# The first products of two kernel generators: three pixel blocks in three column tiles of TensorE, one relu for each three

## Chip, core and metric

The kernel runs on one core of one Trainium2 chip. The metric is the device time of one execution in microseconds. Three runs of the kernel before gave a median of 3211.7 us (3210.56 to 3212.76).

## What is computed

The input `x` is 4 images of 256 channels by 64 x 64 pixels, all in float32. Four layers follow one another, each `x = x + layer(group_norm(x))`: a 3 x 3 convolution with attention over all pixels (layer 0), linear attention (layer 1), a convolution whose weights are generated from the image itself (layer 2), and a mixture of four expert matrices (layer 3). Only the generators of layer 2 are touched here:

```python
def _gen_kernel(x, W1, b1, W2, b2):
    h = relu(einsum('bchw,rc->brhw', x, W1) + b1)     # 8 hidden rows, all 4096 pixels
    pooled = h.mean(axis=(2, 3))
    return pooled @ W2.T + b2
dk = _gen_kernel(x, Wd1, bd1, Wd2, bd2)               # 3x3 weights, one set per channel
pk = _gen_kernel(x, Wp1, bp1, Wp2, bp2)               # 256 x 256 mixing weights
```

The two generators have 8 hidden rows each, so `W1` of both together is 16 rows over 256 channels.

## The kernel before

A channel lies on a partition. 256 channels are two halves `h` of 128 partitions (`NH = 2`), and a half image is 128 x 4096 numbers. An image is worked through in 8 blocks of 512 pixels, the width of one PSUM bank.

The order of the instructions is written out by hand. Layer 0's attention is a generator, `attend` (L610 to L673): each of its steps issues two products `pf` (L620), two exponentials `pr` on ScalarE (L621), two products `py` (L659) that read the exponentials of the step before, and one running sum `tot` on VectorE (L109). What is left of the image before (its layers 1 to 3) and the next image's convolution form a second generator, a `Chain` (L39). `run` (L1096) takes one step of the chain and then one step of the attention, so that both lie in one another's gaps on every engine. A chain's part ends a stretch with `yield n`: about n times a rate makes one step. The rate is 1.5 for the first image's attention, 0.86 for the next two and 1.24 for the last. Images 0, 1 and 2 have their layers 1 to 3 beside the attention of images 1, 2 and 3. Image 3 has no attention left to lie beside: its tail runs alone at the end, with products of image 2's mixing (`held`) put into gaps.

The function touched is `generated` (L855 to L1000), which is layer 2. It scales the 16 columns of `W1` by the group norm's factor (`w1n`, L862), and makes the bias of the hidden rows by four tiny products into `ps_b1` (L866; the profile writes `ps_b`) and a subtraction (`b1n`, L868). Then it goes over 8 blocks of pixels:

```python
for c in range(N // 512):
    ps = bank("ps_h")
    for h in range(NH):
        nc.tensor.matmul(ps[0:2 * R, :], w1n[:, h, :], big[:, h, bass.ts(c, 512)], ...)
    nc.scalar.activation(junk()[0:2 * R, :], ps[0:2 * R, :], AF.Relu, bias=b1n, accum_out=hs[:, c:c + 1])
```

The relu's `accum_out` sums the block's 512 pixels into one column of `hs`. In the same round of the loop one piece of the image is normalised into `xin` (L889 on ScalarE; in the last image every second one is on VectorE, L887), and the round ends with `yield 0.5`. After the loop `hs` is summed to `pooled` (L892), set on the diagonal of `pd` (L894), spread over all partitions by a product with ones (`ps_pool`, L897), and turned into the 3 x 3 weights `dk` by three VectorE operations. These weights start the convolution: ScalarE writes its centre tap (`centre`, L914), and in the last image nine diagonal matrices (L969) before it; VectorE adds the eight other taps (`dw`, L112), and products `ps_pw` (L922) mix the channels.

In front of all that, at the kernel's start, SyncE issues the loads of the weights one after the other (`resident`, L142), GpSimd fills constants, and VectorE makes two averaging matrices (`block_average`, L175) between the statistics of the first image.

Of the kernel before, what the change touches and what calls it, by code (L numbers as in the profile page):

```python
# [8 lines left out]
F32 = mybir.dt.float32  # L9
AF = mybir.ActivationFunctionType  # L10
ALU = mybir.AluOpType
AX = mybir.AxisListType

P = 128
NH = 2
HW = 64
N = HW * HW
# [4 lines left out]
R = 8  # L22
# [11 lines left out]

TY, MY, TX, MX = 6, 4, 4, 2
IY, IX = HW // MY, HW // MX


class Chain:  # L39
# [42 lines left out]
def conv_preact_fast(ctx: ExitStack, tc: tile.TileContext, guard, x, wc, wtpg, ww, wqkv, wout, w1cat, wd2,  # L82
# [3 lines left out]
    nc = tc.nc  # L86
    B = x.shape[0]

    cp = ctx.enter_context(tc.tile_pool(name="const", bufs=1))
    wk = ctx.enter_context(tc.tile_pool(name="work", bufs=1))  # L90
    sp = ctx.enter_context(tc.tile_pool(name="small", bufs=2))
# [7 lines left out]
    def k2(name):  # L99
        return wk.tile([P, 512], F32, tag="k2", name=name, bufs=6)  # L100

    def junk():
        return wk.tile([P, 512], F32, tag="junk", name="junk")

    def bank(name):
        return pp.tile([P, 512], F32, tag="bank", name=name, bufs=8)

    def tt(o, a, b, op):
        nc.vector.tensor_tensor(o, a, b, op)  # L109
# [9 lines left out]
    big = cp.tile([P, NH, N], F32, name="big")  # L119
# [3 lines left out]
    theta, phi, g = tpg[:, 0, :], tpg[:, 1, :], tpg[:, 2, :]  # L123
# [18 lines left out]
    def resident(name, src):  # L142
        t = cp.tile(list(src.shape), F32, name=name)
        nc.sync.dma_start(out=t, in_=src)
        return t
# [8 lines left out]
    ww_s = resident("ww_s", ww)  # L154
    wqkv_s = resident("wqkv_s", wqkv)
    wout_s = resident("wout_s", wout)
    w1_s = resident("w1_s", w1cat)
    b1_s = resident("b1_s", b1cat)
    wd2_s = resident("wd2_s", wd2)
    bd2_s = resident("bd2_s", bd2)  # L160
    rw1_s = resident("rw1_s", rw1)
# [6 lines left out]
    ident = cp.tile([P, P], F32, name="ident")  # L168
    make_identity(nc, ident)
    ones = cp.tile([P, P], F32, name="ones")  # L170
# [4 lines left out]
    def block_average(name, k):  # L175

        member = sp.tile([P, P // k], F32, name=name + "_m", bufs=1)
        nc.vector.tensor_reduce(member, ident.rearrange("p (g k) -> p g k", k=k), AX.X, ALU.add)
        t = cp.tile([P, P], F32, name=name)
        nc.vector.tensor_scalar(t.rearrange("p (g k) -> p g k", k=k),  # L180
                                member.unsqueeze(2).to_broadcast([P, P // k, k]), 1.0 / k, None, ALU.mult)
        return t

    avg32 = block_average("avg32", HD)
    avg8 = block_average("avg8", 8)

    def rsqrt(o, v):
# [85 lines left out]
    def group_finish(st, avg, eps, shift=None):  # L273


        mv = sp.tile([P, NH, 2], F32, name="mv")
        for h in range(NH):
            nc.vector.bn_aggr(mv[:, h, :], st[:, h, :, :].rearrange("p c s -> p (c s)"))
        if shift is not None:
            tt(mv[:, :, 0], mv[:, :, 0], shift, ALU.add)  # L280
        yield 1
        pm = bank("pm")
        nc.tensor.matmul(pm[:, 0:NH], avg, mv[:, :, 0], start=True, stop=True)
        gm = sp.tile([P, NH], F32, name="gm")
        nc.vector.tensor_copy(gm, pm[:, 0:NH])
        ev = sp.tile([P, NH], F32, name="ev")
        tt(ev, mv[:, :, 0], gm, ALU.subtract)
        tt(ev, ev, ev, ALU.mult)
        tt(ev, ev, mv[:, :, 1], ALU.add)
        yield 1  # L290
        pv = bank("pv")
        nc.tensor.matmul(pv[:, 0:NH], avg, ev, start=True, stop=True)
        rstd = sp.tile([P, NH], F32, name="rstd")
        nc.vector.tensor_scalar(rstd, pv[:, 0:NH], eps, None, ALU.add)  # L294
        rsqrt(rstd, rstd)
        return mv, gm, rstd
# [558 lines left out]
    def generated(w, b, big, k4, st, sh, diag):  # L855
        _, gm, rstd = yield from group_finish(st, avg8, 1e-5, sh)
        nb = norm_bias(gm, rstd, sh)
        off = sp.tile([P, NH], F32, name="off")
        tt(off, gm, sh, ALU.subtract)

        w1n = sp.tile([P, NH, 2 * R], F32, name="w1n")
        tt(w1n, w1_s, rstd.unsqueeze(2).to_broadcast([P, NH, 2 * R]), ALU.mult)  # L862
        yield 1
        pb1 = bank("ps_b1")
        for h in range(NH):
            nc.tensor.matmul(pb1[0:2 * R, 0:1], w1n[:, h, :], off[:, h:h + 1], start=(h == 0), stop=(h == NH - 1))  # L866
        b1n = sp.tile([2 * R, 1], F32, name="b1n")
        tt(b1n, b1_s, pb1[0:2 * R, 0:1], ALU.subtract)  # L868
        hs = sp.tile([2 * R, 8], F32, name="hs")
        pk = k2("pk")  # L870
        nc.sync.dma_start(out=pk, in_=bp2)

# [2 lines left out]
            nc.sync.dma_start(out=t, in_=wp2[:, bass.ts(j, 2), :])  # L875
            return t

        for c in range(N // 512):
            ps = bank("ps_h")
            for h in range(NH):  # L880
                nc.tensor.matmul(ps[0:2 * R, :], w1n[:, h, :], big[:, h, bass.ts(c, 512)],  # L881
                                 start=(h == 0), stop=(h == NH - 1))
            nc.scalar.activation(junk()[0:2 * R, :], ps[0:2 * R, :], AF.Relu, bias=b1n, accum_out=hs[:, c:c + 1])
            h, q = c % 2, c // 2
            normed = xin[:, h, bass.ts(q, CH // HW), :], big[:, h, bass.ts(q, CH)].rearrange("p (y x) -> p y x", x=HW)
            if diag is not None and h == 1:
                nc.vector.tensor_scalar(*normed, rstd[:, h:h + 1], nb[:, h:h + 1], ALU.mult, ALU.add)  # L887
            else:
                nc.scalar.activation(*normed, AF.Identity, bias=nb[:, h:h + 1], scale=rstd[:, h:h + 1])  # L889
            yield 0.5  # L890
        pooled = sp.tile([2 * R, 1], F32, name="pooled")
        nc.vector.tensor_reduce(pooled, hs, AX.X, ALU.add)  # L892
        pd = sp.tile([2 * R, 2 * R], F32, name="pd")
        nc.vector.tensor_scalar(pd, ident[0:2 * R, 0:2 * R], pooled, 1.0 / N, ALU.mult, ALU.mult)  # L894
        yield 1
        ppl = bank("ps_pool")
        nc.tensor.matmul(ppl[:, 0:2 * R], ones[0:2 * R, :], pd, start=True, stop=True)  # L897
        pb = sp.tile([P, 2 * R], F32, name="pb")
        nc.vector.tensor_copy(pb, ppl[:, 0:2 * R])
        dkp = k2("dkp")[:, 0:NH * 9 * R].rearrange("p (k r) -> p k r", r=R)  # L900
# [6 lines left out]
        rows = CH // HW  # L907
# [64 lines left out]
        for n, i in enumerate(mine):  # L972
# [15 lines left out]
            c, h = PARTS[i]  # L988
# [86 lines left out]
    def tail(b, big, qT, k4=k4, diag=None, xs_in=None, held=None):  # L1075

        def layers(w):
            st, sh = yield from nonlocal_out(w, b, big, k4, xs_in)
            st = yield from linear_attention(w, b, big, qT, k4, st, sh, diag is not None)
            st, sh = yield from generated(w, b, big, k4, st, sh, diag)  # L1080
            if b + 2 < B:
                load_x(b + 2)
            elif b + 2 == B:
                for h in range(NH):
                    for q in range(2):
                        half_image = bass.ts(q, N // 2)
                        nc.sync.dma_start(out=x_cols[:, h, half_image], in_=xs_d[b + 1, h, :, half_image])
            yield from mixed(w, b, big, k4, st, sh, held)
        return layers
# [557 lines left out]
@with_exitstack  # L1647
def conv_preact_kernel(ctx: ExitStack, tc: tile.TileContext, *args):
    nc = tc.nc
    B = args[0].shape[0]  # L1650
    gp = ctx.enter_context(tc.tile_pool(name="guard", bufs=1))
    guard = gp.tile([P, 2, B * NQ + 1], F32, name="guard")
    conv_preact_fast(tc, guard, *args)


    fit = gp.tile([P, 2, B * NQ + 1], F32, name="fit")
    for side in range(2):
        nc.vector.tensor_scalar(fit[:, side, :], guard[:, side, :], GUARD_MAX[side], None, ALU.is_le)
    low = gp.tile([P, 1], F32, name="low")
    nc.vector.tensor_reduce(low, fit.rearrange("p s k -> p (s k)"), AX.X, ALU.min)  # L1660
    every = gp.tile([P, P], F32, name="every")
    nc.gpsimd.memset(every, 1.0)
    good = gp.tile([P, 1], mybir.dt.int32, name="good")
    with tc.tile_pool(name="guard_ps", bufs=1, space=bass.MemoryType.PSUM) as gps:
        count = gps.tile([P, 1], F32, name="count")
        nc.tensor.matmul(count, every, low, start=True, stop=True)
        nc.vector.tensor_scalar(good, count, P - 0.5, None, ALU.is_ge)
    in_range = nc.values_load(good[0:1, 0:1], min_val=0, max_val=1)
    with tc.If(in_range < 1):
        conv_preact_general(tc, *args)  # L1670
# [58 lines left out]
```

## Time and profile before

| | |
|---|---|
| median of three runs | 3211.7 us |
| the profiled execution | 3210.14 us, of which its span is 3208.4 us |
| TensorE (PE) busy | 3071.0 us, 96% of the span |
| VectorE (DVE) busy | 2075.8 us, 65% |
| ScalarE (ACT) busy | 1146.0 us, 36% |
| GpSimd (POOL) busy | 129.4 us, 4% |
| mean granted TensorE clock | 0.986 of full |

A line of a group or of the timeline names the source line, the engine, the operation, what it writes and reads, and how many instructions were merged. A float32 product leaves two weight loads (PEld) and two matmul records (PE), one for each of two passes: the 64 products of `ps_h` show as 128 records. In a dense row the records of matmuls overlap (those of `ps_h` last 592 ns each and start 0.43 us apart), so what a pass occupies is read from the distance between starts. In the timeline, `[1.30 <-PE ps_h L881]` says that the engine had been idle for 1.30 us before the line, and what ended it. L109 and L112 are the helpers `tt` and `stt`, so that VectorE's work is told apart by the tile's name.

### The profile page before, as it was taken

The numbers are of one execution on the slowest core, as the hardware profiler recorded it, in microseconds if no ns is written. First come the engines' busy times: TensorE is split into PE (matmuls) and PEld (weight loads), VectorE is DVE, ScalarE is ACT, GpSimd is POOL, SyncE is SP. The second block draws the span as 40 slices with busy tenths as digits, with TensorE's granted clock in tenths as the row PEclk, the third lists the DMA queues.
The fourth block names the chain that finished last, engine by engine and source line by source line (L and its number), as shares of the span: only waits on it lengthen the run. The fifth ranks groups of instructions, "written<-read, shape, count | busy, mean of one in ns | idle before, by whom it ended". The sixth has DMA issues, their size and how long they took to land.

```text
span 3208.4 us, 24196 instructions
## 1 busy us (share of the span) xinstructions
PE 3071.0 (96%) x8494; PEld 1476.7 (46%) x8494; DVE 2075.8 (65%) x2603; ACT 1146.0 (36%) x2139; POOL 129.4 (4%) x169
## 2 busy tenths in 40 slices
PE   6899999999999999999999999999999999996797
PEld 3354444445564444444565444444555534443533
DVE  8636776443556986876537796878353768855575
ACT  2133224333555332223364432312355443333520
POOL 0000000000010000000011000000000100000100
PEclk9999999999999999999999999999999999998998
DMA  5510113001100023113200102210510010121101
GB/s 180 173 39 27 33 34 62 7 13 63 49 10 27 13 72 118 40 33 76 101 11 6 35 20 90 101 38 27 129 42 1 10 40 7 49 70 46 50 0 73
DMA packets 73792, 161.66 MB, mean 50 GB/s; under 512 B 7744, under 2 KB 39232, under 8 KB 70720
## 3 DMA queue, kind: packets, MB, share of 16 engines
q1 hardware_dynamic: 69056, 143.27, 13.1%
q0 software_dynamic: 4608, 16.78, 2.9%
q8 instruction: 69, 1.13, 0.2%
q14 instruction: 59, 0.48, 0.0%
HBM read 103.40 MB, written 73.40 MB: 55 GB/s over the span
## 4 chain that ended last, share of the span: by engine, by line
PE 79%; DVE 12%; issue 5%; ACT 2%; DMA 0%; POOL 0%; SPq 0%; POOLq 0%; ACTq 0%
PE pf L620 23%; PE py L659 23%; PE ps_conv L382 8%; PE ps_qkv L748 5%; DVE dw L112 4%; PE ps_tp L596 3%; PE ps_ex L1059 3%; PE ps_pw L922 2%; DVE tot L109 2%; PE ps_g L601 2%; PE ps_h L881 2%; PE ps_wy L643 2%; PE ps_o L813 1%; PE ps_ctx L768 1%; PE ps_ss L735 1%
## 5 line engine op out<-in xcount | busy, mean ns | idle before, releaser
L621 ACT ACTIVATE pr<-pf 128x512 f32<-128x512 f32 x1024 | 604.1, 596 | 1227.7 <-PE pf L620 1203.7
L620 PE MATMUL pf<-tpg 128*128 128x512 f32 x2048 | 968.7, 595 | 1.4 <-ACT pr L621 1.4
L659 PE MATMUL py<-pr,tpg 128*128 128x512 f32 x2048 | 962.1, 592 | 3.0 <-ACT pr L621 2.9
L109 DVE TENSOR_TENSOR tot<-tot,pr 128x1024 f32<-128x1024 f32 x448 | 546.5, 1220 | 263.3 <-ACT pr L621 261.7
L659 PEld LDWEIGHTS py<-pr,tpg 128*128 128x128 f32 x2048 | 388.8, 190 | 494.2 <-issue 478.3
L620 PEld LDWEIGHTS pf<-tpg 128*128 128x128 f32 x2048 | 381.6, 190 | 447.3 <-issue 419.2
L112 DVE SCALAR_TENSOR_TENSOR dw<-xp,dk,dw 128x1008 f32<-128x1008 f32 x224 | 283.1, 1268 | 7.0 <-ACT dw L914 3.7
L382 PE MATMUL ps_conv<-v,u 128*128 128x512 f32 x576 | 260.7, 599 | 12.7 <-issue 9.0
L382 PEld LDWEIGHTS ps_conv<-v,u 128*128 128x128 f32 x576 | 110.3, 192 | 154.0 <-issue 147.0
L748 PE MATMUL ps_qkv<-wqkv_s,xg 128*128 128x384 f32 x384 | 130.7, 490 | 0.0
L596 PE MATMUL ps_tp<-big,wtpg_s 128*128 128x512 f32 x256 | 116.8, 599 | 3.0 <-ACT big L471 3.0
L189 POOL TENSOR_TENSOR rstd<-rstd,half 128x2 f32<-128x2 f32 x24 | 16.8, 701 | 2478.8 <-DVE rstd L294 2285.2
L109 DVE TENSOR_TENSOR tpg<-ps_g,bg_s 128x512 f32<-128x512 f32 x32 | 22.1, 692 | 144.3 <-PE ps_g L601 144.3
L922 PE MATMUL ps_pw<-dw,pk 128*128 128x512 f32 x224 | 103.8, 597 | 10.9 <-DVE dw L112 10.9
L634 DVE RECIPROCAL inv<-pss 128x512 f32<-128x512 f32 x32 | 107.2, 3351 | 7.3 <-PE pss L632 7.3
L748 PEld LDWEIGHTS ps_qkv<-wqkv_s,xg 128*128 128x128 f32 x384 | 72.2, 190 | 52.5 <-issue 8.9
L756 DVE TENSOR_REDUCE qs<-qk 128x16 f32<-128x512 f32 x24 | 16.5, 686 | 123.4 <-ACT qk L750 123.4
L109 DVE TENSOR_TENSOR v<-ra 128x1024 f32<-128x1024 f32 x72 | 86.7, 1220 | 0.4
L597 ACT ACTIVATE tpg<-ps_tp,btp_s 128x512 f32<-128x512 f32 x64 | 43.7, 686 | 118.4 <-PE ps_tp L596 118.4
L922 PEld LDWEIGHTS ps_pw<-dw,pk 128*128 128x128 f32 x224 | 42.7, 191 | 65.4 <-issue 50.9
L596 PEld LDWEIGHTS ps_tp<-big,wtpg_s 128*128 128x128 f32 x256 | 47.5, 193 | 54.3 <-issue 49.8
L750 ACT ACTIVATE qk<-ps_qkv,rinv 128x256 f32<-128x256 f32 x96 | 45.4, 473 | 74.2 <-PE ps_qkv L748 71.2
(273 smaller groups left out, 2948.2 us busy)
## 6 DMA issues: line engine op xcount, KB each, us to landing
u<-filters SPq DMA_DIRECT2D x144, 128.0 KB, 2.3
xp<-in_x_dram SPq DMA_DIRECT2D x16, 1024.0 KB, 6.4
xs_d<-big POOLq DMA_DIRECT2D x32, 512.0 KB, 11.3
wy_d<-wt SPq DMA_DIRECT2D x32, 512.0 KB, 3.0
out_dram<-res SPq DMA_DIRECT2D x64, 256.0 KB, 2.0
wy<-wy_d SPq DMA_DIRECT2D x28, 512.0 KB, 5.1
xs<-xs_d SPq DMA_DIRECT2D x24, 512.0 KB, 5.3
wp<-in_wp_dram SPq DMA_DIRECT2D x16, 512.0 KB, 4.6
```

The source lines that it names most:

```text
L109: nc.vector.tensor_tensor(o, a, b, op)
L112: nc.vector.scalar_tensor_tensor(o, a, s, b, op0, op1)
L382: nc.tensor.matmul(ps[oh], u(oh, h), v[:, bass.ts(h, 512)], start=(h == 0), stop=(h == NH - 1))
L596: nc.tensor.matmul(ps, wtpg_s[:, h, k, :], big[:, h, cols], start=(h == 0), stop=(h == NH - 1))
L601: nc.tensor.matmul(ps[:, j, :], big[:, h, bass.ts(4 * c + j, P)], wtpg_s[:, h, 2, :], start=(h == 0), stop=(h == NH - 1))
L620: nc.tensor.matmul(pf, phi[:, bass.ts(2 * m + s, P)], theta[:, bass.ts(q, 512)], start=True, stop=True)
L621: nc.scalar.activation(pr[:, bass.ts(s, 512)], pf, AF.Exp)
L634: nc.vector.reciprocal(inv, pss)
L659: nc.tensor.matmul(py, g[:, bass.ts(2 * m + s, P)], probs[i][:, bass.ts(s, 512)], start=(m == 0 and s == 0), stop=(m == NM - 1 and s == 1))
L748: nc.tensor.matmul(ps[:, 0:3 * HID], xg[:, h, bass.ts(j, P)], wqkv_s[:, h, :], start=(h == 0), stop=(h == NH - 1))
L922: nc.tensor.matmul(ps, pk[:, h * NH * P + oh * P:h * NH * P + (oh + 1) * P], dw[h][:, bass.ts(s, 512)], start=(h == 0), stop=(h == NH - 1))
L1059: nc.tensor.matmul(ps, wm[h][:, bass.ts(oh, P)], big[:, h, cols], start=(h == 0), stop=(h == NH - 1))
```

## The change

The 8 blocks are taken in three groups of 3, 3 and 2 (`HT = 3`). The blocks of one group write to one PSUM bank, at partitions 0, 32 and 64, so that each uses another 32 columns of the array. For this the 16 columns of `W1` are padded with zeros to 32 (`HP`). The order within a group is: half 0 of each block, then half 1 of each block. One relu reads the 96 partitions (64 in the last group) of a group and sums into one column of `hs`, which is now 96 x 3 and is zeroed by GpSimd beforehand. The groups are issued in rounds 0, 1 and 2 of the loop over the 8 pieces; the rounds' normalisations and yields stay.

Around it: the bias products are made three times, once for each column tile (6 in place of 2 for each image). `pooled` and `pd` have 96 partitions, and `pd` is made with a new constant `same`, three 16 x 16 identities one below the other with gaps, so that the product with ones also adds up the three tiles. At the kernel's start there are two more memsets on GpSimd, a load of `W1` in 16-number pieces, two more loads of the bias on SyncE's queue, and two VectorE additions for `same` ahead of the averaging matrices.

```diff
+HP, HT = 32, 3
+NC3 = -(-N // 512 // HT)
...
-    w1_s = resident("w1_s", w1cat)
-    b1_s = resident("b1_s", b1cat)
+    w1_s = cp.tile([P, NH, HP], F32, name="w1_s")
+    b1_s = cp.tile([HT * HP, 1], F32, name="b1_s")
+    nc.gpsimd.memset(w1_s, 0.0)
+    nc.gpsimd.memset(b1_s, 0.0)
+    nc.sync.dma_start(out=w1_s[:, :, 0:2 * R], in_=w1cat)
+    for t in range(HT):
+        nc.sync.dma_start(out=b1_s[t * HP:t * HP + 2 * R, :], in_=b1cat)
...
+    same = cp.tile([HT * HP, 2 * R], F32, name="same")
+    tt(same, ident[0:HT * HP, 0:2 * R], ident[0:HT * HP, HP:HP + 2 * R], ALU.add)
+    for t in range(2, HT):
+        tt(same, same, ident[0:HT * HP, t * HP:t * HP + 2 * R], ALU.add)
...
-        w1n = sp.tile([P, NH, 2 * R], F32, name="w1n")
+        w1n = sp.tile([P, NH, HP], F32, name="w1n")
...
+        hs = sp.tile([HT * HP, NC3], F32, name="hs")
+        nc.gpsimd.memset(hs, 0.0)
         yield 1
         pb1 = bank("ps_b1")
-        for h in range(NH):
-            nc.tensor.matmul(pb1[0:2 * R, 0:1], w1n[:, h, :], off[:, h:h + 1], start=(h == 0), stop=(h == NH - 1))
...
+        for t in range(HT):
+            for h in range(NH):
+                nc.tensor.matmul(pb1[bass.ts(t, HP), 0:1], w1n[:, h, :], off[:, h:h + 1], start=(h == 0), stop=(h == NH - 1))
+        b1n = sp.tile([HT * HP, 1], F32, name="b1n")
+        tt(b1n, b1_s, pb1[0:HT * HP, 0:1], ALU.subtract)
...
-        for c in range(N // 512):
+        def hidden(g):
+            blocks = list(range(g * HT, min((g + 1) * HT, N // 512)))
             ps = bank("ps_h")
             for h in range(NH):
-                nc.tensor.matmul(ps[0:2 * R, :], w1n[:, h, :], big[:, h, bass.ts(c, 512)],
-                                 start=(h == 0), stop=(h == NH - 1))
-            nc.scalar.activation(junk()[0:2 * R, :], ps[0:2 * R, :], AF.Relu, bias=b1n, accum_out=hs[:, c:c + 1])
+                for t, c in enumerate(blocks):
+                    nc.tensor.matmul(ps[bass.ts(t, HP), :], w1n[:, h, :], big[:, h, bass.ts(c, 512)],
+                                     start=(h == 0), stop=(h == NH - 1))
+            rows = slice(0, len(blocks) * HP)
+            nc.scalar.activation(junk()[rows, :], ps[rows, :], AF.Relu, bias=b1n[rows, :], accum_out=hs[rows, g:g + 1])
+
+        for c in range(N // 512):
+            if c < NC3:
+                hidden(c)
             h, q = c % 2, c // 2
...
-        pd = sp.tile([2 * R, 2 * R], F32, name="pd")
-        nc.vector.tensor_scalar(pd, ident[0:2 * R, 0:2 * R], pooled, 1.0 / N, ALU.mult, ALU.mult)
+        pd = sp.tile([HT * HP, 2 * R], F32, name="pd")
+        nc.vector.tensor_scalar(pd, same, pooled, 1.0 / N, ALU.mult, ALU.mult)
         yield 1
         ppl = bank("ps_pool")
-        nc.tensor.matmul(ppl[:, 0:2 * R], ones[0:2 * R, :], pd, start=True, stop=True)
+        nc.tensor.matmul(ppl[:, 0:2 * R], ones[0:HT * HP, :], pd, start=True, stop=True)
```

On TensorE the instructions of an image's loop then stand as follows, between the attention's steps (a bracket is one stretch of `ps_h` products):

| image | before | after |
|---|---|---|
| 0 and 1 | [2] [6] [4] [4] | [6] [10] |
| 2 | [2] [2] [4] [4] [2] [2] | [6] [6] [4] |
| 3 (alone) | [16] | [16] |

On ScalarE the relus of images 0 and 1 are three in the first two steps, and the eight normalisations stand after them as before: 1, 3, 2 and 2 of them in four steps. In image 3 ScalarE's order was relu, piece, two relus, piece, two relus, piece, two relus, piece, relu; it becomes relu, piece, two relus, three pieces.

## Prediction

> **What bounds the kernel now.** I read the page's busy shares first, then the tile `ps_h`, then the busy times by stage, then the timeline of one step and of the last image. TensorE is busy 96% of the span:
>
> ```profile
> PE 3071.0 (96%) x8494; PEld 1476.7 (46%) x8494; DVE 2075.8 (65%) x2603; ACT 1146.0 (36%) x2139; POOL 129.4 (4%) x169
> ```
>
> The share alone doesn't say that the touched stage is bound by TensorE. The stretch of image 0's loop and the 150 us around it do (columns: PE, PEld, DVE, ACT, POOL busy):
>
> ```profile
> 996.90:1027.70 30.80, 30.80 (x75) 9.66 (x74) 9.49 (x11) 20.28 (x36) 0.00 (x0) 1.00 0.16 51
> 1000.00:1150.00 150.00, 149.59 (x348) 62.43 (x347) 125.92 (x124) 66.79 (x110) 0.00 (x0) 1.00 0.07 25
> ```
>
> TensorE never stops there; ScalarE and VectorE have room. Image 2's stretch (2545 to 2600) and all stages up to 2850 are also fully busy, so TensorE time removed there passes to the end.
>
> What one product costs is read from the starts:
>
> ```profile
> 1009.42 1.98 PE L620 MATMUL pf<-tpg 128*128 128x512 f32 x4
> ...
> 1013.05 3.61 PE L881 MATMUL ps_h<-big,w1n 128*16 128x512 f32 x8
> 1013.49 0.10 PEld L881 LDWEIGHTS ps_h<-big,w1n 128*16 128x16 f32 x1 [0.33 <-issue]
> 1013.92 0.10 PEld L881 LDWEIGHTS ps_h<-big,w1n 128*16 128x16 f32 x1 [0.33 <-issue]
> ...
> 1016.59 1.98 PE L620 MATMUL pf<-tpg 128*128 128x512 f32 x4
> ```
>
> A weight load every 0.43 us, so 0.43 us a pass and 0.86 us a product of two passes, whether 16 or 128 columns are used. From one `pf` to the next lie 7.17 us with 8 products (4 of the attention, 4 of `ps_h`). 8 x 0.86 is 6.88, so a stretch of `ps_h` costs another 0.29 us. Image 2's stretches of two agree: 5.45 us from 2562.56 to 2568.01 for 6 products, 0.29 over.
>
> The last image stands alone, and its products are on the path:
>
> ```profile
> 3045.79 15.80 PE L881 MATMUL ps_h<-tpg,w1n 128*16 128x512 f32 x32
> 3061.78 0.66 ACT L883 ACTIVATE junk<-ps_h,b1n 16x512 f32<-16x512 f32 x1
> 3062.57 0.15 DVE L892 TENSOR_REDUCE pooled<-hs 16x1 f32<-16x8 f32 x1 [13.57 <-ACT junk L883]
> 3064.63 1.57 ACT L969 ACTIVATE tpg<-ident,dk 128x128 f32<-128x128 f32 x5 [2.09 <-DVE dk L109]
> ```
>
> ScalarE's diagonals wait for the last relu and 2.1 us of small steps. The first five passes take 0.855 us each at a lower granted clock (0.78 on average from 3040 to 3070).
>
> **What the Trainium skill says.** "TensorE: Matmul & The Clock Gate", section "Measured speedup vs the span model", gives 2.38 times for three column tiles of 32 columns and 512 pixels. No run here shows it, and none shows column tiles side by side at all. The same page, "The mechanism", says that matmuls start and end in program order, and "Step-by-step: what each phase is for" that only weight loads are pulled ahead; the trace agrees as far as it goes, with one load during each pass before. "TensorEngine Tiling (Array Packing)", "Key Properties", says that a change of the tiling mode drains the array, while another tile of the same mode doesn't. The 0.29 us around each stretch, in which the weights of `pf` aren't loaded ahead, fit that; so the kernel before already pays for the mode.
>
> **The change, part by part.**
>
> *How far three tiles overlap* is the unknown. A float32 product is two passes, A1 A2 of one tile, then B1 B2, then C1 C2. A2 needs A's columns and must wait for A1. B1 can start with A2, as it uses other columns; B2 can't start before B1 ends, and by then C1 starts with it. If starts stay in order, two passes run side by side, never three: n products take n+1 passes of 0.43 us, not 2n. That is my case, about two times, less than the page's 2.38. Bounds: 2.38 times, 0.36 us a product, at the good end; nothing gained, 0.86 us, at the bad end, and below nothing in the last rival.
>
> *Images 0 and 1.* Before: 16 x 0.86 + 4 stretches x 0.29 = 14.9 us. After, stretches of 6 and 10: (7 + 11) x 0.43 + 2 x 0.29 = 8.3. Each saves 6.6.
>
> *Image 2.* Before: 13.8 + 6 x 0.29 = 15.5. After, 6, 6, 4: (7 + 7 + 5) x 0.43 + 3 x 0.29 = 9.0. Saves 6.5. The three save 19.7 us of TensorE, which has no gap to swallow them.
>
> *Does ScalarE become late?* Five relus fewer, at 0.87 us (0.68 and 0.19 for the sum), save 4.3 us an image, but the eight pieces of 1.23 us stay. From the start of image 0's second stretch (time 0): its groups end at 3.0 and 4.8; relu to 3.9, piece to 5.1, relu to 6.0, two pieces to 8.5, exponentials (1.05 a pair) to 9.6, two pieces and exponentials to 13.1, again to 16.6. `py` needs these three pairs at 9.9, 13.4 and 17.0. The margin is 0.3 to 0.4 us; I put down up to 1 us of new stalls in all. The centre taps queued behind wait for `dk` anyway. VectorE is idle before `dk` (7.5 us before `pooled` in image 2), so its taps start earlier by as much as TensorE gains.
>
> *Image 3.* 17 passes in place of 32. From 3046.0 some five of 0.855 at the lower clock and 12 of 0.43: groups all out at about 3055.5, last relu to 3056.4. `dk` would be ready 2.0 later, but three pieces now stand behind that relu on ScalarE: 3 x 1.14 to 3059.8, and the diagonals start there, not at 3064.6. Saves 4.8 us, where 6.1 would come without the pieces. Next late are the diagonals and centre, as before.
>
> *Bias products.* The first `ps_h` matmul starts 0.11 us after the first of four `ps_b` passes (996.90 to 997.01), so 27 ns a pass. Eight more passes cost 0.22 us, 0.7 for three images; image 3's are in its sum. Bounds: 0.4 and 4 in all.
>
> *Small widenings.* `w1n` 128x64 in place of 128x32, `pd`, `pooled`, and the zeroing of `hs` (GpSimd is idle 8.95 us before `rstd`; it stands behind that on the queue and long before the first relu): nothing. A load of 32 columns, between 97 ns for 16 and 190 ns for 128, hides under a pass of 430. `b1n` waits behind the reciprocal on VectorE until 999.8 as before, and the first group now ends about 1000.3, later than that.
>
> *Start.* VectorE runs without a gap from 5.99 to 16.7, and two additions (0.15 us, as `b1n`) go into that: 0.3 us on the path. Two memsets (about 0.2 us) stand before the identity on GpSimd, ready at 1.8 and needed at 8.4: covered. SyncE's two more loads cost 0.35 us each behind 18.9; filters written after 30 us don't wait for them. Uncovered they would be 0.7.
>
> *Sum.* 19.7 + 4.8 - 0.7 - 0.3 - 1.0 = 22.5 us. The profiled execution took 3210.1 us (span 3208.4 and 1.7 around it): 3187.6. The median stands 1.6 higher: 3189.
>
> **Rivals.**
>
> *Weights are loaded only when the pass before starts.* B1 then begins a load (0.11 us) after A2: 0.54 us a product. Three images save 5.7 + 5.7 + 6.0, the last 3.7; less 1 to 2: about 3192. For it: the trace shows loads exactly one pass ahead. I count it with the forecast, two streams: together 0.65.
>
> *Three side by side* at the page's rate, 0.36 us a product: 8.5 + 8.5 + 8.9 + 5.8, less 1.0, and about 1 us of waiting for exponentials in each image, since ScalarE needs 3.6 us a step against 3.44 of TensorE: 3183. For it: the page; against it: two passes a product, in order. 0.15.
>
> *The change doesn't do what it says*: float32 products in other columns aren't overlapped. Then seven stretches fewer save 2.0, and bias, start and the pieces behind the last relu (1.4) cost 2.4: 3212. 0.12.
>
> *Slower: each change of the column tile drains the array*, as the mode's change does. Half of 0.29 for each of 64 products is 9.3, for 24 bias products 3.5, and the 0.4 above: 3225. It decides from about 0.07 us a change without overlap. Against it: the page on tiles of one mode. 0.08.
>
> **The numbers.** About 0.2%, 6.4 us, is what a measurement of this kernel tells from no change. Two streams and three hold 0.80, so the range is theirs with the bounds of bias and stalls, and room for a weaker overlap of 1.4 times (16 x 0.61 us): 3181 to 3203. Faster 0.80, same 0.12, slower 0.08.
>
> **What would show it.** Right: `ps_h` starts in pairs, stretches of 6 near 3.3 us and of 10 near 5.0; image 3's products over 9 to 10 us, its diagonals about 5 us earlier against `ps_b`. Wrong: a start every 0.43 us (no overlap), gaps between starts (drain), `py` idle for `pr` (ScalarE late), or an end that doesn't move by what the stretches gained.

## The result, and the profile after

| | before | after |
|---|---|---|
| median of four runs beside each other | 3212.09 us | 3174.9 us (3174.41 to 3175.83) |
| the profiled execution, its span | 3210.14 us, 3208.4 us | 3175.36 us, 3173.5 us |
| TensorE busy | 3071.0 us | 3035.6 us |

The ratio is 0.9885, with an interval of 0.9868 to 0.9902. The forecast of 3189 had the sign right and the size wrong: the kernel gained 37 us where 22.5 were expected, and the time lies 6 us below the range. The two profiled executions are 34.8 us apart, because that of the kernel before was 2.0 us quicker than its median and that of the kernel after 0.5 us slower; the parts below are read from these two. The first lines of the two profiles already say where the gain is: TensorE is busy for 35.4 us less and still for 96% of the span, so the removed time went through to the end.

```profile
PE 3035.6 (96%) x8526; PEld 1472.2 (46%) x8526; DVE 2075.4 (65%) x2605; ACT 1132.1 (36%) x2099; POOL 129.6 (4%) x175
```

The timeline of image 0's loop in the kernel after has the answer. The columns are start, length, engine, line, operation and tiles.

```profile
997.86 0.31 PE L886 MATMUL ps_b<-off,w1n 128*32 128x1 f32 x12
998.00 1.91 PE L903 MATMUL ps_h<-big,w1n 128*32 128x512 f32 x12
999.84 1.98 PE L637 MATMUL pf<-tpg 128*128 128x512 f32 x4
...
1005.19 3.63 PE L903 MATMUL ps_h<-big,w1n 128*32 128x512 f32 x20
```

The stretch of six products runs from 998.00 to the next `pf` at 999.84: 1.84 us. The stretch of ten runs from 1005.19 to 1008.75: 3.56 us. With 4 and 8 passes of 0.43 us, rather than the 7 and 11 of the prediction, both leave the same 0.12 us, the part of a border (0.29 in all) that lies between the last pass and the next `pf`. Four passes for six products of two passes are two products one after the other in each tile, and three tiles at once. The weight loads show it directly:

```profile
997.97 0.17 PEld L903 LDWEIGHTS ps_h<-big,w1n 128*32 128x32 f32 x6
998.44 0.14 PEld L903 LDWEIGHTS ps_h<-big,w1n 128*32 128x32 f32 x3 [0.29 <-issue]
998.87 0.14 PEld L903 LDWEIGHTS ps_h<-big,w1n 128*32 128x32 f32 x3 [0.29 <-issue]
```

Six loads go out together (the first and second pass of each of three tiles), and then three at every further pass. The rows below are the whole span, cut at the same instructions in both profiled executions:

| part of the span, us | before | after | gain |
|---|---|---|---|
| start to image 0's `ps_b` | 996.90 | 997.86 | -0.96 |
| image 0, `ps_b` to `ps_pool` | 30.49 | 21.29 | 9.20 |
| image 1, the same | 30.49 | 21.29 | 9.20 |
| image 2, the same | 41.39 | 31.93 | 9.46 |
| image 3, `ps_b` to the first `ps_dw` | 20.59 | 13.29 | 7.30 |
| the three parts between them | 1946.39 | 1947.14 | -0.75 |
| first `ps_dw` to the end | 142.1 | 140.7 | 1.4 |

The four loops give 35.2 us. What is left between, ahead and behind adds up to -0.3. These shifts of up to 1.4 us lie where TensorE runs at half its pace for a time (see "The border").

Image 3 in the kernel after, from its products to the diagonals:

```profile
3019.74 7.27 PE L903 MATMUL ps_h<-tpg,w1n 128*32 128x512 f32 x32
...
3027.12 0.68 ACT L906 ACTIVATE junk<-ps_h,b1n 64x512 f32<-64x512 f32 x1 [0.93 <-PE ps_h L903]
...
3027.80 3.49 ACT L916 ACTIVATE xp<-tpg,nb,rstd 128x1024 f32<-128x1024 f32 x3
...
3029.85 0.18 DVE L114 TENSOR_TENSOR dk<-dk,bd_s 128x18 f32<-128x18 f32 x1
3031.19 2.14 ACT L996 ACTIVATE tpg<-ident,dk 128x128 f32<-128x128 f32 x7
```

The products take 7.27 us, where 15.80 were needed. As predicted, the three pieces queued behind the last relu end after `dk` is ready (3030.03), and the diagonals wait for them until 3031.19.

### The profile page after: what moved, and what is told of

Its sections match the earlier page's. It is cut to its first block, busy times and chain, and to the rows that moved or that the text cites. A ratio compares the mean times of both kernels' runs of the same rounds, so it can differ in the third digit from the quotient of the medians.

```text
span 3173.5 us, 24226 instructions
## 1 busy us (share of the span) xinstructions
PE 3035.6 (96%) x8526; PEld 1472.2 (46%) x8526; DVE 2075.4 (65%) x2605; ACT 1132.1 (36%) x2099; POOL 129.6 (4%) x175
## 4 chain that ended last, share of the span: by engine, by line
PE 79%; DVE 13%; issue 5%; ACT 2%; DMA 0%; POOL 0%; SPq 0%; POOLq 0%; ACTq 0%
PE pf L637 23%; PE py L676 23%; PE ps_conv L399 8%; PE ps_qkv L765 5%; DVE dw L117 4%; PE ps_tp L613 4%; PE ps_ex L1086 3%; PE ps_pw L949 3%; DVE tot L114 2%; PE ps_g L618 2%; PE ps_wy L660 2%; PE ps_o L830 1%; PE ps_ctx L785 1%; PE ps_ss L752 1%; PE pss L649 1%
## 5 line engine op out<-in xcount | busy, mean ns | idle before, releaser
L832 ACT ACTIVATE junk<-ps_o 128x256 f32<-128x256 f32 x128 | 49.2, 384 | 63.6 <-PE ps_o L830 60.6
```

## The experiments

Each kernel is the one after with the edit shown, unless the text says otherwise; ratios are to the kernel before, run on the same chip. Two questions had to be told apart. Why do three tiles run fully side by side, when the prediction expected two? And is the gain that of the tiles, or does it come from the fewer relus and stretches?

### All blocks in one tile

```diff
-        hs = sp.tile([HT * HP, NC3], F32, name="hs")
+        hs = sp.tile([HT * HP, 8], F32, name="hs")
...
-            ps = bank("ps_h")
+            ps = [bank("ps_h") for _ in blocks]
...
-                    nc.tensor.matmul(ps[bass.ts(t, HP), :], w1n[:, h, :], big[:, h, bass.ts(c, 512)],
+                    nc.tensor.matmul(ps[t][0:HP, :], w1n[:, h, :], big[:, h, bass.ts(c, 512)],
...
-            rows = slice(0, len(blocks) * HP)
-            nc.scalar.activation(junk()[rows, :], ps[rows, :], AF.Relu, bias=b1n[rows, :], accum_out=hs[rows, g:g + 1])
+            for t, c in enumerate(blocks):
+                nc.scalar.activation(junk()[0:HP, :], ps[t][0:HP, :], AF.Relu, bias=b1n[0:HP, :], accum_out=hs[0:HP, c:c + 1])
```

> The changed kernel with all blocks on the first column tile: the same order and the same two or three stretches, but three banks and three relus a group. Theory S: all overlap is gone, a product takes 0.86 us again; images 0 and 1 cost 14.3 us in place of 5.4, image 2 14.6 in place of 5.5, image 3 about 8 more; 3208 to 3212, so the merged stretches alone are worth 0 to 4 us. Theory R (the gain comes from the order, fewer stretches or fewer instructions elsewhere): 3195 or less.

Measured: 3213.29 against 3211.39, ratio 1.0005 (0.9996 to 1.0014). The order of the products and the stretches are those of the kernel after; only the tile is one, each block has a bank of its own, and the relus are eight. Its timeline for image 0:

```profile
999.08 5.32 PE L903 MATMUL ps_h<-big,w1n 128*32 128x512 f32 x12
1004.33 1.98 PE L637 MATMUL pf<-tpg 128*128 128x512 f32 x4
...
1009.68 8.77 PE L903 MATMUL ps_h<-big,w1n 128*32 128x512 f32 x20
1018.38 0.70 PE L637 MATMUL pf<-tpg 128*128 128x512 f32 x1
```

The six products take 5.25 us here and 1.84 us in three tiles, the ten 8.70 and 3.56. The fewer stretches save 0.65, 0.65 and 0.93 us in the loops of images 0, 1 and 2 (29.84, 29.84 and 40.46 us), about 0.29 for each border gone, and image 3 gives 1.2 of it back (`ps_b` to `ps_dw` 21.77 for 20.59) through the pieces behind the last relu. Without tiles beside one another the total shows no gain.

### Both halves of a block one after the other

```diff
-            for h in range(NH):
-                for t, c in enumerate(blocks):
+            for t, c in enumerate(blocks):
+                for h in range(NH):
```

> The changed kernel with the order inside a group turned: both halves of block A, then both of B, then both of C, so that a tile's second product stands directly behind its first. Theory S (each column tile runs its own products, and a product that waits for its tile holds no other tile up): the stretches stay at 1.84 us for 6 products and 3.56 for 10, and the time stays at 3175, within 2 us. Theory O (products start in the order in which they stand, and the changed kernel gains only because neighbours in its order lie on different tiles): A's second product must wait for two passes and B stands behind it; a stretch of 6 takes 8 to 10 passes, 3.4 to 4.4 us, one of 10 takes 5.7 to 7, and the time goes to 3190 to 3198.

Measured: 3176.82 against 3211.39, ratio 0.9892 (0.9876 to 0.9909). The program's order is now A A B B C C, if A, B and C are the tiles. With starts in that order B's first product could start only when A's second one does, at pass 3, and C's at pass 5, eight passes for the six. The trace of this kernel:

```profile
997.28 0.18 PEld L903 LDWEIGHTS ps_h<-big,w1n 128*32 128x32 f32 x6
997.75 0.15 PEld L903 LDWEIGHTS ps_h<-big,w1n 128*32 128x32 f32 x3 [0.28 <-issue]
```

```profile
997.31 1.92 PE L903 MATMUL ps_h<-big,w1n 128*32 128x512 f32 x12
999.16 1.98 PE L637 MATMUL pf<-tpg 128*128 128x512 f32 x4
```

Again six loads within 0.18 us and three at each later pass, and 1.85 us from the first product to the next `pf`. B and C start while a whole product of A, which stands ahead of them, still waits. So starts in different column tiles are not held to the program's order, neither pass by pass nor product by product.

### Two and four tiles

```diff
-HP, HT = 32, 3
+HP, HT = 32, 2
```

> The changed kernel with two column tiles in place of three: four groups of 2, so stretches of 4 and 12 products in images 0 and 1, of 4, 4 and 8 in image 2. Theory S in its simplest form (a stretch lasts as many passes of 0.43 us as its busiest tile has, and 0.12 more to the next pf): 1.84 and 5.28 us, 1.84, 1.84 and 3.56; 1.7 us more an image than with three tiles, and the same in image 3: 3181 to 3184. If a part of the gain doesn't scale with the number of tiles (a fixed gain of the mode, or of the order): 3175 to 3178.

Measured: 3185.27 against 3211.92, ratio 0.9919 (0.9902 to 0.9935); the loops of images 0 to 2 are 1.8 us longer than with three tiles, as expected, image 3's part only 0.9 longer where 1.7 were expected. The total lies above the expected 3181 to 3184 all the same: in the profiled execution another 3.1 us are lost outside the loops, 1.0 between them and 2.1 in the last part. The second stretch of image 0, with twelve products:

```profile
1005.22 5.34 PE L903 MATMUL ps_h<-big,w1n 128*32 128x512 f32 x24
1010.50 0.70 PE L637 MATMUL pf<-tpg 128*128 128x512 f32 x1
```

```diff
-HP, HT = 32, 3
+HP, HT = 32, 4
```

> Four column tiles in place of three (a fourth at partition 96), two groups of 4, one relu over 128 partitions. Theory S with nothing special about three: 8 products take the 1.84 us of two, an image's two stretches 3.7 us in place of 5.4, so 1.7 us less in each of four images: 3167 to 3170. If three tiles are the most that run side by side (four moving streams too many, or the fourth tile waits): 8 products take 2.7 us or more, and the time stays at 3174 or above.

Measured: 3171.17 against 3211.39, ratio 0.9876 (0.986 to 0.9893), 1.2 us above the expected range. The parts with the loops are 1.7, 1.7, 2.0 and 1.5 us shorter than with three tiles, as expected; the parts between them are 1.9 us longer. Its timeline for image 0, the second stretch with eight products in four tiles:

```profile
1004.11 1.92 PE L903 MATMUL ps_h<-big,w1n 128*32 128x512 f32 x16
1005.96 1.12 PE L637 MATMUL pf<-tpg 128*128 128x512 f32 x2
```

Eight products take 1.85 us with four tiles; six take 1.84 us with three; the twelve with two tiles take 5.28 us, 12 x 0.43 and the same 0.12. The overlap is full at every count: a pass of 0.43 us serves as many products as there are tiles. The fourth tile, at partition 96, runs like the others.

### How far ahead it looks: the order of products in four tiles

If a waiting product of A doesn't hold up B, how many can wait? One stretch with all 16 products of an image, four tiles, two banks, one relu for each bank, and three orders. In the first, all four products of a tile stand together:

```diff
-HP, HT = 32, 3
+HP, HT = 32, 4
...
-                    nc.tensor.matmul(ps[bass.ts(t, HP), :], w1n[:, h, :], big[:, h, bass.ts(c, 512)],
...
+            ps = [bank("ps_h") for _ in range(NC3)]
+            for t in range(HT):
+                for k in range(NC3):
+                    for h in range(NH):
+                        nc.tensor.matmul(ps[k][bass.ts(t, HP), :], w1n[:, h, :], big[:, h, bass.ts(k * HT + t, 512)],
...
-            if c < NC3:
+            if c == 0:
```

> Four column tiles, all 16 products of an image in one stretch and tile by tile: four products (eight passes) of tile A, then four of B, of C, of D, so that D's first pass stands behind 24 others. If TensorE looks as far ahead as that: one stretch of 8 passes, 3.56 us, and the time is that of the four tiles above or 0.5 less, 3169 to 3172. If its view ends sooner: B, C and D start late, the stretch takes 4.5 us or more (up to 13.9 without any overlap), and the time rises by 1 us or more in each image, 3175 to 3210.

Measured: 3191.77 against 3211.92, ratio 0.9936 (0.992 to 0.9953). With four products of a tile in a row most of the overlap is gone. The loads of this kernel show where B, C and D come in:

```profile
998.96 0.11 PEld L903 LDWEIGHTS ps_h<-big,w1n 128*32 128x32 f32 x1
...
1000.25 0.11 PEld L903 LDWEIGHTS ps_h<-big,w1n 128*32 128x32 f32 x1 [0.32 <-issue]
1000.68 0.14 PEld L903 LDWEIGHTS ps_h<-big,w1n 128*32 128x32 f32 x3 [0.32 <-issue]
...
1002.43 0.14 PEld L903 LDWEIGHTS ps_h<-big,w1n 128*32 128x32 f32 x3 [0.32 <-issue]
...
1004.17 0.14 PEld L903 LDWEIGHTS ps_h<-big,w1n 128*32 128x32 f32 x3 [0.32 <-issue]
```

A's passes start at 998.96, 999.39, 999.82, 1000.25 and 1000.68; B's first two loads appear at the fifth, when A's third product starts and its fourth is the only one that waits. From that I took a rule: each tile has one product running and one waiting, and the first product that finds both places of its tile taken holds up everything behind it. It gives 20 passes for this order (B at pass 5, C at 9, D at 13, and D's four products until 20), and the trace has C's first loads at 1002.43 and D's at 1004.17, 8 and 12 passes after 998.96. The stretch takes 8.77 us, 998.96 to 1007.73, for 20 x 0.43 = 8.6 and a part of the border. Two other orders test the rule with numbers given beforehand: pairs of each tile, and threes.

```diff
+            order = [(t, k, h) for k in range(NC3) for t in range(HT) for h in range(NH)]
+            for t, k, h in order:
...
-            if c < NC3:
+            if c == 0 and diag is None:
...
+        if diag is not None:
+            hidden(0)
```

> Four column tiles, all 16 products of an image in one stretch, by pairs: both halves of a block stand one behind the other (A A B B C C D D, then the same for the second four blocks), and image 3 has its pieces ahead of the relus. Theory Q (each tile has one product running and one waiting, and the first product that finds both places of its tile taken holds up all behind it): no product of the first eight finds both places taken, and the next A is held up only until A has a place free: 8 passes, 3.56 us for the stretch, one border of 0.29 us less an image than with two stretches; images 0 and 1 from ps_b to ps_pool 19.3 us, the time 3168 to 3171. If a product can't wait at a busy tile without holding up the others: 5 us or more for the stretch, 3174 or more.

```diff
+            order = [(t, k, h) for t in range(HT) for k, h in ((0, 0), (0, 1), (1, 0))] + [(t, 1, 1) for t in range(HT)]
+            for t, k, h in order:
```

> Four column tiles, one stretch, with three products of a tile in a row (A A A B B B C C C D D D, then A B C D). Theory Q: the third A waits outside until A's first is done, so B starts with pass 2, C with 4, D with 6, and D's fourth product ends after 14 passes: 14 x 0.43 + 0.12 = 6.1 us from the first ps_h to the next pf, 2.7 us less an image than with four in a row (8.77), and 3179 to 3184 for the kernel. If what can be looked past is a number of passes and not of places at each tile: 15 passes or more, 6.5 us.

Measured: pairs 3170.6 against 3212.46, ratio 0.987 (0.9853 to 0.9886); threes 3181.78 against 3212.46, ratio 0.9904 (0.9888 to 0.9921). In the timelines, first of pairs and then of threes, the stretch ends where `pf` begins:

```profile
998.33 3.66 PE L902 MATMUL ps_h<-big,w1n 128*32 128x512 f32 x31
1001.91 0.70 PE L637 MATMUL pf<-tpg 128*128 128x512 f32 x1
```

```profile
999.55 0.14 PEld L902 LDWEIGHTS ps_h<-big,w1n 128*32 128x32 f32 x3 [0.32 <-issue]
```

```profile
999.12 5.83 PE L902 MATMUL ps_h<-big,w1n 128*32 128x512 f32 x31
1004.88 1.56 PE L637 MATMUL pf<-tpg 128*128 128x512 f32 x3
```

Pairs: 998.32 (the first record, on a line of its own) to 1001.91, 3.59 us, 8 passes. Threes: 998.68 to 1004.88, 6.20 us for the 14 passes that the rule gives; B's two loads come with A's third pass (999.55), when A's third product finds a place. The rule held in both. What these orders can't tell is its unit: a product here is two passes, and a limit of four passes for each tile, one running and three waiting, gives the same 8, 14 and 20 (a limit of three gives 11, 17 and 23, one of five 8, 11 and 17).

### One relu for each block

```diff
-            rows = slice(0, len(blocks) * HP)
-            nc.scalar.activation(junk()[rows, :], ps[rows, :], AF.Relu, bias=b1n[rows, :], accum_out=hs[rows, g:g + 1])
+            for t in range(len(blocks)):
+                rows = bass.ts(t, HP)
+                nc.scalar.activation(junk()[rows, :], ps[rows, :], AF.Relu, bias=b1n[rows, :], accum_out=hs[rows, g:g + 1])
```

> The changed kernel with one relu for each block (32 partitions each) in place of one for each group: eight relus an image again, the column tiles kept. Theory S (the gain is TensorE's time): the stretches stay at 1.84 and 3.56 us; ScalarE has 4.3 us more an image and lets the attention's second product wait by 1 to 2 us in images 0 and 1, the last image loses 0.9; 3178 to 3181. Theory R (much of the gain beyond my sum, 14 of 37 us, comes from the merged relu and a freer ScalarE): 3187 or more.

Measured: 3184.57 against 3211.39, ratio 0.9918 (0.9902 to 0.9935). That is 9.7 us above the median of the kernel after and falls between what was expected of either theory. In the two profiled executions 8.15 us lie between them: 1.7 and 2.0 in images 0 and 1, none in image 2, 3.4 in image 3 (0.9 were expected there), and 1.1 outside the loops, 1.6 more in the last part and 0.5 less ahead and between. In images 0 and 1 `py` waits for exponentials again:

```profile
1015.25 1.13 PE L676 MATMUL py<-pr,tpg 128*128 128x512 f32 x2 [1.38 <-ACT pr L638]
```

In image 3 the relus stand one behind the other on ScalarE:

```profile
3031.19 0.68 ACT L907 ACTIVATE junk<-ps_h,b1n 32x512 f32<-32x512 f32 x1
...
3031.99 0.68 ACT L907 ACTIVATE junk<-ps_h,b1n 32x512 f32<-32x512 f32 x1
```

One starts every 0.80 us, so three blocks take 2.4 us where TensorE now gives them in 1.72 (four passes): ScalarE becomes the bound of image 3's loop. The merged relu costs the same 0.68 and 0.19 us over 96 partitions. This kernel and the one with all blocks in one tile have the same order of products and eight relus an image each; they differ by the tiles and banks, and by 28.7 us in the median (3184.57 and 3213.29). So the tiles give most of the gain without the merged relu. The merged relu keeps ScalarE from taking a part of it back.

### The border: 66 columns in the kernel before

This one is the kernel before, with its 16 columns padded with zeros to 66, still one block after the other:

```diff
-    w1_s = resident("w1_s", w1cat)
+    w1_s = cp.tile([P, NH, 66], F32, name="w1_s")
+    nc.gpsimd.memset(w1_s, 0.0)
+    nc.sync.dma_start(out=w1_s[:, :, 0:2 * R], in_=w1cat)
...
-            nc.tensor.matmul(pb1[0:2 * R, 0:1], w1n[:, h, :], off[:, h:h + 1], start=(h == 0), stop=(h == NH - 1))
+            nc.tensor.matmul(pb1[0:66, 0:1], w1n[:, h, :], off[:, h:h + 1], start=(h == 0), stop=(h == NH - 1))
...
-                nc.tensor.matmul(ps[0:2 * R, :], w1n[:, h, :], big[:, h, bass.ts(c, 512)],
+                nc.tensor.matmul(ps[0:66, :], w1n[:, h, :], big[:, h, bass.ts(c, 512)],
```

> The kernel before with W1 padded by zeros to 66 columns, so that its products take the whole width of the array like pf and py and no longer the narrow tile; everything else as before, products one after the other. If the 0.29 us around each stretch is the change of the tiling mode (the array drains, and the next weights aren't loaded ahead): it goes, pf to pf over 8 products takes 6.88 us and not 7.17, and 14 stretches save 4.1 us: 3206 to 3209. If it comes from anything else at the border (another accumulator, the semaphores): 7.17 stays, and 3211 with it.

Measured: 3212.39 against 3211.92, ratio 1.0003 (0.9994 to 1.0011). The mechanism was right and the total was missed. In its timeline:

```profile
1009.57 1.88 PE L622 MATMUL pf<-tpg 128*128 128x512 f32 x4
...
1013.00 3.60 PE L883 MATMUL ps_h<-big,w1n 128*66 128x512 f32 x8
...
1016.01 0.19 PEld L622 LDWEIGHTS pf<-tpg 128*128 128x128 f32 x1 [0.29 <-ACT junk L885]
1016.44 1.02 PE L622 MATMUL pf<-tpg 128*128 128x512 f32 x2
```

From `pf` to `pf` are 6.87 us, 8 x 0.86, where the kernel before has 7.17, and the weights of `pf` are loaded a pass ahead (1016.01). The border of 0.29 us is gone when the product is too wide for a small tile, which fits the prediction's reading of it as a change of mode; widths between 32 and 66 columns weren't run. The three images' loops are 0.97, 0.97 and 1.57 us shorter, 3.5 in all. The gain didn't reach the end: the parts between the loops were 3.5 us longer and the last part 1.8.

Of this, 2.1 us lie between image 2's `ps_pool` and image 3's `ps_b`, where both kernels have the same instructions. Laid side by side, the two traces keep step to 0.1 us until the products `ps_qkv`. There the kernel with 66 columns falls 1.2 us behind, and 0.8 more at `ps_zt` and `ps_o`. First the kernel before, then this one:

```profile
2936.78 7.21 PE L748 MATMUL ps_qkv<-wqkv_s,ra 128*128 128x384 f32 x16
...
3013.90 1.60 PEld L813 LDWEIGHTS ps_o<-w,tpg 128*128 128x128 f32 x8
```

```profile
2935.08 8.36 PE L750 MATMUL ps_qkv<-wqkv_s,ra 128*128 128x384 f32 x16
...
3013.86 2.73 PEld L815 LDWEIGHTS ps_o<-w,tpg 128*128 128x128 f32 x8
```

The passes of `ps_qkv` start 0.64 us apart at first and 0.32 us apart later, in both; here three to four more of them have the longer distance. So the time is lost to stretches at half the pace, which fall on other work in the two executions. The mean granted clock says the same: from 2930 to 2945 it is 0.77 in the kernel before and 0.63 in this one, from 3011 to 3018 it is 1.00 and 0.76.

The shifts between the kernel before and the kernel after, outside the loops, arise in the same way. At the start, `ps_row` begins at 25.63 and 25.57; its passes go from 0.85 us apart to 0.43 later in the kernel after, which costs it 0.6 us, and `ps_tp` (eight records in 5.25 and in 5.60 us) costs the rest of the 0.96. Of the parts between the loops, `ps_conv` costs the kernel after 1.0 us ahead of image 2 and saves 0.3 ahead of image 1. In the last part, the passes of `ps_ex` stay 0.85 us apart for longer in the kernel before. What decides where such a stretch begins and ends was not found.

### Image 3's pieces ahead of its products

The kernel with four tiles, and in the last image all the pieces issued ahead of the two relus:

```diff
-            if c < NC3:
+            if c < NC3 and diag is None:
...
+        for g in range(NC3 if diag is not None else 0):
+            hidden(g)
```

> Four column tiles, and in image 3 alone ScalarE's four pieces stand before the relus and not behind the last one. If the pieces behind the last relu hold up the diagonals, as the prediction said: from ps_pool to the first ps_dw 3.0 us in place of 4.3, image 3 about 1.3 us shorter, 3168 to 3170. If the diagonals wait for dk anyway, or if the pieces now hold up the first relu: no difference, 3171.

Measured: 3170.37 against 3211.92, ratio 0.987 (0.9853 to 0.9886). ScalarE in image 3:

```profile
3017.62 4.64 ACT L916 ACTIVATE xp<-tpg,nb,rstd 128x1024 f32<-128x1024 f32 x4 [8.99 <-DVE nb L114]
...
3026.42 1.86 ACT L998 ACTIVATE tpg<-ident,dk 128x128 f32<-128x128 f32 x6 [2.11 <-DVE dk L114]
```

The diagonals wait for `dk` again, not for pieces, and `ps_b` to `ps_dw` takes 10.20 us where four tiles alone take 11.82. The 1.6 us can be seen there and not in the median, which lies only 0.8 us below that of four tiles alone and just above the 3168 to 3170 of the first expectation. The four-tile kernels that lose nothing to their order (this one, the plain one and pairs) have medians of 3170.4 to 3171.2, and gain 40 to 42 us over the kernel before, where the kernel after gains 37; they can't be told from one another.

## Why the prediction was wrong, point by point

- **The failed step** is "If starts stay in order, two passes run side by side, never three: n products take n+1 passes". Measured are 4, 8 and, in image 3, 12 passes where it gives 7, 11 and 17: the third tile doesn't start a pass late, its first matmul record begins 0.03 us after that of the first tile (998.00 to 998.03). I had taken a sentence of the Trainium skill ("TensorE: Matmul & The Clock Gate", "The mechanism", matmuls start and end in program order) and applied it to the passes of a float32 product, of which it doesn't speak. For the order of the kernel after, products that start in order would have given the measured time too. The halves one after the other show that products don't keep it either across column tiles, so there the measurement decides against the page. "TensorEngine Tiling (Array Packing)", "Key Properties", which I had read for the drain alone, also says that different tiles run their loads and matmuls in parallel; the runs agree.
- **The term that was mis-sized by it**, worked again with the passes measured: images 0 and 1 take 12 x 0.43 + 0.58 = 5.7 in place of 14.9, so 9.2 each (measured 9.20); image 2 takes 12 x 0.43 + 0.87 = 6.0 in place of 15.5, so 9.5 (9.46); image 3's products take 5 x 0.855 + 7 x 0.43 = 7.3 (7.27). The 19.7 us of the prediction become 27.9. In image 3 five passes fewer than it counted are another 2.15, so its 4.8 become 6.95 (measured 7.30).
- **The rival "three side by side"** had the mechanism and got 0.15. It took 2.38 times from the Trainium skill; here it was 3.0 in a dense row (the 12 passes of six products in the time of 4). Its waiting for exponentials, 1 us an image, didn't come.
- **Product and border**: 0.86 and 0.29 us were right; the border was confirmed by taking it away.
- **New stalls**, -1.0: none. `py` starts 1.7 to 1.8 us after `pf` throughout image 0's loop, as it would without any wait, and in the profile the idle time of `py` that `pr` ends is 2.9 us in both kernels. That ScalarE was near its limit was right: with one relu a block, `py` waits 1.38 us for it in image 0.
- **Bias**, -0.7: the first `ps_h` starts 0.14 us after the first `ps_b` where it was 0.11, so 0.03 us an image. (Before, these were two products of two passes each; the text ahead of the prediction calls them four products.) The price of 27 ns a pass didn't hold for twelve passes. These products lie in different tiles too, which may be why; it was not tried.
- **Image 3's pieces**: right, 1.16 us (3031.19 less 3030.03) for 1.3 to 1.4.
- **Start**, -0.3: not paid. `ps_row`, the first long row of products, begins 0.06 us earlier than before. Image 0's `ps_b` is 0.96 later all the same, through the two stretches at half the pace that are named under "The border". That is read from the traces and not tried by an experiment.
- **The sum** with the measured passes is 9.2 + 9.2 + 9.5 + 6.95, less 0.1 for the bias, 34.8 us, and gives 3175.4 for the profiled execution, which took 3175.36. That it comes out so closely is partly luck: image 3 gained 0.35 more than in this sum, and the parts outside the loops lost 0.3.

## What to carry to other kernels

Products that use few columns are cheap to put side by side: with the output at partition 0, 32, 64 and 96 of one bank, as many run in one pass's time as there are tiles, as long as no tile has more than two products in a row in the program. This was shown for float32 products of 512 pixels over all 128 rows; for a type that takes one pass, how many may stand in a row is open. Merge what reads the bank as well, since the next engine then gets its work several times as fast. A statement on order should be tried on the unit that one's own data type makes (here two passes), with the other unit kept as a rival of weight.

## What the runs showed of the hardware that was not expected

- Column tiles overlap fully: 512 pixels in two passes take 0.86 us, whether one, two, three or four tiles work.
- Each tile takes one running and one waiting product (or four passes, which is the same here); a third one in a row blocks all others behind it until the first is done (16 products in 3.59, 6.20 and 8.77 us for pairs, threes and fours).
- A stretch of products of 16 or 32 columns costs 0.29 us going in and out among wide ones, even when they all use the first tile; with 66 columns the cost is gone.
- A few us taken out of a busy loop can be lost elsewhere: 3.5 us out of the loops with 66 columns left the total as it was, because products elsewhere ran at half the pace for longer (`ps_qkv` 8.36 us for 7.21).
